# One LayerNorm pass for two in the first stage of a decoder layer, and its splits into high and low parts shared out anew over three engines

## The chip, the cores and the metric

The kernel runs on one core of one Trainium2 chip. The metric is the device time of one execution in microseconds (us); the figure for the kernel before is the median of three runs. A profiled execution beside them gives the trace that all views are drawn from. Five engines work side by side, each in the order of its own list of instructions: PE (TensorE: matmuls; its weight loads are shown as PEld), DVE (VectorE), ACT (ScalarE), POOL (GpSimd) and SP (SyncE, which here issues DMAs).

## The reference, cut to what matters

Inputs are `x` (2 x 2048 tokens of 512 channels), a context, weights. Three blocks follow one another, each on a LayerNorm of its input and added to it: an attention over the rows of two weight matrices, an attention over the context, and a feed-forward part with 32 experts. The change concerns the first block alone:

```
m  = mean(x);   v  = var(x)                      # of each token
r  = (x - m) / sqrt(v + 1e-5)                    # outer LayerNorm
y  = (r - mean(r)) * rsqrt(var(r) + 1e-5)        # inner LayerNorm
q  = (y * ln_g + ln_b), four heads of 128
s  = q @ w_fc.reshape(-1, 128).T                 # 2048 keys for every head
p  = relu(s) ** 2
x1 = x + r + p @ w_proj.T.reshape(-1, 128)
```

The variance of r is v / (v + 1e-5) and its mean is 0. So y is (x - m) times a function of v alone, and x + r is x times one factor plus one offset for each token.

## The kernel before, in words

The program has stages one after another: `stage0` (the block above), `stage1` (attention over the context, and the router), the shared expert, the routed experts. In the profile `stage0` runs from the start to about 822 us of 2793.

**Numbers in parts.** Matmuls take float32r operands. To keep float32 accuracy an operand x is split (`split`, lines 88 to 91 of the listing, L90 and L91 in the profile) into a high part, a cast to float32r, and a low part, x minus the high part; a product is then three matmuls, lo x hi, hi x lo, hi x hi (`three`). In `split` the cast is always on ACT; the subtraction is on DVE, or on POOL where the caller says so.

**Order of the work.** The kernel is written as a list of statements; a scheduler with a model of the engines' times fixes each engine's order when the program is built. `g.after(...)` makes what is emitted within stand behind the named instructions on their engines, `later` lowers the priority. Nothing is reordered at run time.

**stage0.** T = 4096 tokens are worked off in eight tiles t of 512. For each tile there are 4 heads h and 16 blocks kt of 128 keys, so 512 steps (t, h, kt), 64 in a tile. A step has

- three matmuls of 128 x 512 for the scores s (L328), into one of four PSUM banks;
- a relu on ACT (L332, tile rl), and p = s times rl on DVE (L334, tile p, three buffers H);
- the split of p into ph and pl (L339: the cast on ACT, the subtraction on POOL for odd steps and on DVE for even ones);
- the three matmuls with the values (`av`, L289), done for the step LAG = 7 steps earlier.

At the end of a head o is copied by ACT (L293); at the end of a tile it is transposed by PE (L302), x1 is read back, the result added by DVE (L303) and written.

**The LayerNorms** (`prep`, L223 to L259) of tile t + 1 are made during tile t, as two generators of two 128-row tiles each (t = 0: one of four). One generator step is taken per step of the loop from kt = 7 of head 0 on. For each 128-row tile: bn_stats and bn_aggr on DVE (L147, L148); for both together the reciprocal deviation (`rstd`, L132 to L136), a power on POOL and a Newton step in small instructions on DVE; r on DVE (L154); x + r on POOL (L234), written to x1 by SP (L235); then the same statistics of r again, a second `rstd`, a small product nb (L246), and y on ACT (L254). In tile 0 two of the four y are on DVE, and the four x + r stand behind the second power on POOL.

`prep_head` (L261) then transposes y for one head on PE (L264), applies gain and bias on ACT (L266, tile q) and splits q. At the start, before the loop, come the LayerNorms of tile 0, its four heads, and the splits of the two weights: kw (low parts all on POOL) and vw (low parts on DVE, behind `g.mark`, the last y on DVE).

**Background.** From tile 1 on, a step of `context_steps` is taken twice per head: the context's keys and values, and the splitting of further weights (wk, ctx, wv, wq, wo; low parts on POOL).

Of the kernel before, what the change touches and what calls it, by code (L numbers as in the profile page):

```python
# [22 lines left out]
C = 512  # L23
# [5 lines left out]
# Tokens that the expert of each rank (by its number of tokens) has a place for, in blocks of 128 and a last one of 64.  # L29
# [4 lines left out]
# Any further tokens go to blocks of one expert each, worked off in a loop of dynamic length.  # L34
NOV = 64
NBLK = NB + NOV
# Blocks of 128 hidden units of the shared expert that are worked off before the routed ones; the others go between those.
HID = 6
# [6 lines left out]
class Ctx:  # L45
    """The chip's memory in tags that all stages share. Tiles of [128, 512]: A .. K."""
# [25 lines left out]
    def after(self, *instructions):  # L72
        """What is emitted within comes behind these on their engines."""
        stack = ExitStack()
        for i in instructions:
            stack.enter_context(self.tc.issue_after(i.ins))
        return stack


@contextmanager  # L80
def later(g, n):
    """What is traced within stands as far back among the engines' work as if n instructions preceded it."""
    g.tc.cur_priority += n
    yield
    g.tc.cur_priority -= n


def split(g, hi, lo, src, lo_engine=None):
    """src = hi + lo exactly, hi and lo in float32r."""
    g.nc.scalar.copy(hi, src)  # L90
    (lo_engine or g.nc.vector).tensor_tensor(lo, src, f32(hi), A.subtract)  # L91


def split_steps(g, dram, hi, lo, lo_engine=None):
    """A matrix as high and low parts hi[k][c] and lo[k][c] of each 128 rows and their columns, step by step."""
    for k in range(len(hi)):
        at = 0
        for h, l in zip(hi[k], lo[k]):
            n = h.shape[-1]
            raw = g.raw.tile([128, n], F32, name="raw", tag="raw")  # L100
            g.nc.sync.dma_start(raw[:], dram[k * 128:(k + 1) * 128, at:at + n])
            split(g, h, l, raw[:], lo_engine)
            at += n
        if at > 256 or k % 2:
            yield
# [8 lines left out]
def part(w, k, c):  # L114
    """128 columns of 128 rows."""
    return w[k][c // 4][:, c % 4 * 128:c % 4 * 128 + 128]


def run(steps):
    """All of the steps at once, and what they return."""  # L120
    try:
        while True:
            next(steps)
    except StopIteration as end:
        return end.value


def rstd(g, var, n, name):
    """(var + EPS) ** -0.5, a power corrected by a Newton step."""
# [10 lines left out]
def ln_stats(g, xs, name):  # L140
    """Means and reciprocal deviations of the rows of n [128, C] tiles: [128, n, 2] and [128, n], step by step."""
    nc = g.nc
    n = len(xs)
    mv = g.sm.tile([128, n, 2], F32, name=name + "m", tag=name + "m")
    for i, x in enumerate(xs):
        s6 = g.small(name + "s", 6)
        nc.vector.bn_stats(s6[:], x)  # L147
        nc.vector.bn_aggr(mv[:, i, :], s6[:])  # L148
        yield
    return mv, rstd(g, mv[:, :, 1], n, name)  # L150
# [6 lines left out]
def three(terms):  # L157
    """The products of high and low parts that count, smallest first: (w, x) pairs."""
    (wh, wl), (xh, xl) = terms
    return (wl, xh), (wh, xl), (wh, xh)  # L160


# ---------------------------------------------------------------- keys and values of the context
def context_steps(g, ctxT, wk, wv, wq, wo, kst, vst):
    """Keys of two heads as the two blocks of a diagonal, high and low parts of the values side by side; and
    the weights that the attention over them starts with."""
# [46 lines left out]
# ---------------------------------------------------------------- attention over the weights' rows  # L213
def stage0(g, x, wfcT, wpT, lnT, x1, background):
# [8 lines left out]
    def prep(t, tiles):  # L223
        """The steps of two LayerNorms of some 128 tokens each; the first only loads them."""
        rows = [slice(t * 512 + s * 128, t * 512 + s * 128 + 128) for s in tiles]
        xt = [g.tile("G", "xt") for _ in rows]
# [3 lines left out]
        mv, rs = yield from ln_stats(g, [v[:] for v in xt], "a")  # L230
        rt = []

        def add(i):
            nc.gpsimd.tensor_tensor(xt[i][:], xt[i][:], rt[i][:], A.add)  # L234
            nc.sync.dma_start(x1[rows[i], :], xt[i][:])  # L235

        for i, v in enumerate(xt):
            r = g.tile("C", "r")
            normalise(g, r[:], v[:], mv, rs, i)
            rt.append(r)  # L240
            if t > 0:
                add(i)
            yield
        mv, rs = yield from ln_stats(g, [v[:] for v in rt], "b")
        nb = g.small("nb", len(rt))
        nc.vector.scalar_tensor_tensor(nb[:], mv[:, :, 0], -1.0, rs[:], A.mult, A.mult)  # L246
        for i, r in enumerate(rt):
            y = r
            if t == 0:
                y = g.tile("DI"[i % 2], "y")  # L250
            if t == 0 and i % 2:
                g.mark = normalise(g, y[:], r[:], mv, rs, i)
            else:
                nc.scalar.activation(y[:], r[:], AF.Identity, bias=nb[:, i:i + 1], scale=rs[:, i:i + 1])  # L254
            ys[t] = ys.get(t, []) + [y]
        if t == 0:
            with g.after(g.pow):
                for i in range(4):
                    add(i)  # L259

    def prep_head(t, h):  # L261
# [4 lines left out]
        nc.scalar.activation(q[:], pt[:], AF.Identity, bias=gb[:, 1, h:h + 1], scale=gb[:, 0, h:h + 1])  # L266
# [4 lines left out]
    run(prep(0, range(4)))  # L271
    prep_head(0, 0)
    kw = run(weight_steps(g, wfcT, 4, 512, "kw", nc.gpsimd))
    prep_head(0, 1)
    with g.after(g.mark):
# [33 lines left out]
    for i, (t, h, kt) in enumerate(steps):  # L309
# [29 lines left out]
        split(g, ph[:], pl[:], p[:], nc.gpsimd if i % 2 else None)  # L339
# [6 lines left out]
# ---------------------------------------------------------------- attention over the context, router  # L346
def stage1(g, x1, mask, kst, vst, gate, x2, zT, xs, ef, background):
# [4 lines left out]
    def transposed(rows, name, tags="BBEF", banks=("P4", "P4")):  # L352
        """High and low parts of the transpose of two [128, C] tiles: hi[c][:, k, :] has rows 256 c + 128 k of it."""
# [11 lines left out]
    def prep(t):  # L365
        """Loads, then the LayerNorm, then its transpose."""
# [79 lines left out]
    def turn(t, q4):  # L446
        """Probabilities of two pairs of heads transposed."""
# [12 lines left out]
    def values(t, q4, h):  # L460
        """Of one head of each pair: high and low parts of its values are side by side in one operand."""
# [18 lines left out]
    def outputs(t, q4):  # L480
        """The part of the output's product that comes from two pairs of heads."""
# [9 lines left out]
    def finish(t):  # L491
        """What comes of the output, step by step."""
# [91 lines left out]
# ---------------------------------------------------------------- where each token goes  # L584
def bc(ap, axis, n):
    """A broadcast dimension of n at that place of [128, k]."""
# [4 lines left out]
def route(g, ef, tab, tri, ids, plan, idx):  # L591
    """Lists of tokens by block: expert of each rank, expert of each further block, their number."""
# [34 lines left out]
    # Rows of each tile before a token with its expert, and of all tiles before it.  # L627
# [14 lines left out]
    # Experts by their number of tokens.  # L642
# [12 lines left out]
    # Blocks beyond those places, and where each expert's begin.  # L655
# [17 lines left out]
    # Of each token: its block and its place therein.  # L673
# [37 lines left out]
# ---------------------------------------------------------------- the expert of all tokens  # L711
def shared_weights(g, wg, wu, wd):
    """Of the layer's first HID blocks of 128 hidden units as pieces of 512 or 256 columns, and of its rest."""
# [74 lines left out]
# ---------------------------------------------------------------- the rest of the expert of all tokens  # L788
class Rest:
    """The steps of its work on the b-th 256 tokens."""  # L790
# [59 lines left out]
# ---------------------------------------------------------------- the experts of a part of the tokens  # L850
def routed(g, xs, rest, plan, idx, wg, wu, wd, out):
# [10 lines left out]
    # The tags that weights come from in turn: of hidden units, of the output, and as they are loaded.  # L862
# [25 lines left out]
    # Of two blocks of 128 tokens the hidden layer is made in its transpose, with the weights as the standing operand.  # L888
    # Of a block of 64 tokens the high and low parts stand side by side as one operand of 128 columns, so that
    # two passes make all products; the results of the parts are added as they leave the PSUM.  # L890
# [9 lines left out]
    def turned(x, m, bank, tags):  # L900
        """The transpose of [m, 512] in high and low parts, by pieces of 128 rows: two operands, or one of both."""
# [111 lines left out]
    # Units of the shared expert's rest stand between experts: their weights need no loading.  # L1013
# [80 lines left out]
# ---------------------------------------------------------------- blocks beyond the experts' places  # L1094
# [46 lines left out]
def constants():  # L1141
    """Tables that depend on shapes alone."""
# [11 lines left out]
def build(tc, I, out):  # L1154
    from contextlib import ExitStack
    nc = tc.nc
    with ExitStack() as outer:
# [11 lines left out]
        with ExitStack() as inner:  # L1169
            g = Ctx(tc, inner)  # L1170
            g.ident = ident[:]
            g.mhalf = g.c.tile([128, 4], F32, name="mhalf")
# [51 lines left out]
```

## Time and profile before

| | us |
|---|---|
| runs | 2786.57, 2788.44, 2792.36 |
| median | 2788.44 |
| span of the profiled execution, first to last instruction | 2793.2 |
| busy in the span: PE | 2690.4 (96%) |
| DVE | 2071.6 (74%) |
| ACT | 1845.3 (66%) |
| POOL | 962.1 (34%) |
| busy from 36 to 780 us: PE | 719.9 of 744 |
| DVE | 641.9 |
| ACT | 613.4 |
| POOL | 435.9 |
| mean granted clock of PE | 0.990 |

For the profiled execution the profile gives the span only, no time of its own beside it; the span lies 4.8 us above the median of the runs and 0.8 above the slowest of them. A matmul's record ends where a model puts it: full matmuls of 512 columns start 0.227 us after each other but show some 0.39 us each, so a busy share of PE hides short gaps, and the number of entries in a stretch tells more. Some records of matmuls can be missing.

Durations of single instructions in `stage0`, mean of the group, 128 x 512 unless said:

| instruction | engine | ns |
|---|---|---|
| p, L334 | DVE | 684 |
| pl, L91 (256 of them) | DVE | 792 |
| pl, L91 (256 of them) | POOL | 1345 |
| ph cast, L90 | ACT | 621 |
| relu, L332 | ACT | 601 |
| bn_stats, L147 | DVE | 680 and 673 |
| r, L154 | DVE | 778, median 543 |
| y, L254 | ACT | 807 |
| x + r, L234 | POOL | 1451 |
| power of 128 x 2, L133 | POOL | 959 and 860 |

### The profile page before, as it was taken

What the parts mean: (1) busy time and instruction counts of PE and PEld (TensorE: products, weight loads), DVE (VectorE), ACT (ScalarE), POOL (GpSimd) and SP (SyncE); (2) the same over time, 40 slices, a digit from 0 to 9 for tenths busy, and PEclk for the clock granted to TensorE, in tenths of its full rate; (3) what the DMA queues carried; (4) which work ended last, traced back from release to release, by engine and by line L of the source; (5) the groups of instructions that cost most, each with busy time, mean ns of one, the idle gap of its engine ahead of it and who ended that gap; (6) DMA issues with size and microseconds to landing.
All of it is one profiled execution on the core that took longest, in us unless ns stands there. A gap on an engine that the chain in (4) does not pass through costs nothing. (4 is left out here: it accounts for less than half of the span.)

```text
span 2793.2 us, 47704 instructions
## 1 busy us (share of the span) xinstructions
PE 2690.4 (96%) x14788; PEld 2308.8 (83%) x14788; DVE 2071.6 (74%) x4765; ACT 1845.3 (66%) x4089; POOL 962.1 (34%) x774
## 2 busy tenths in 40 slices
PE   5999999999999999999999999999999999999997
PEld 4877877877878999899988888888888988887786
DVE  8898888888887888888877522145677677778885
ACT  5887887887867777777774111135566666667774
POOL 5475465566543333333330120002122222222222
PEclk9999999999999999999999999999999999999999
DMA  3022122122120223222245322255788889988994
GB/s 132 23 76 72 65 69 69 65 62 75 36 81 21 88 74 115 92 85 77 84 144 184 110 91 86 90 175 157 255 275 268 271 270 286 285 268 260 298 304 143
DMA packets 238002, 396.71 MB, mean 142 GB/s; under 512 B 29376, under 2 KB 67280, under 8 KB 237744
## 3 DMA queue, kind: packets, MB, share of 16 engines
q1 hardware_dynamic: 223024, 366.45, 39.4%
q0 software_dynamic: 14720, 27.19, 5.1%
q8 instruction: 117, 1.92, 0.3%
q14 instruction: 141, 1.16, 0.1%
HBM read 311.67 MB, written 83.83 MB: 142 GB/s over the span
## 5 line engine op out<-in xcount | busy, mean ns | idle before, releaser
L91 DVE TENSOR_TENSOR rl<-raw,rh 128x512 fp32r<-128x512 f32 x768 | 513.8, 713 | 134.5 <-ACT rh L90 129.5
L90 ACT CAST rh<-raw 128x512 fp32r<-128x512 f32 x768 | 447.4, 621 | 159.0 <-DMA raw<-in_rg 97.7
L91 POOL TENSOR_TENSOR pl<-p,ph 128x512 fp32r<-128x512 f32 x256 | 344.2, 1345 | 301.0 <-ACT ph L90 282.1
L334 DVE TENSOR_TENSOR p<-s,rl 128x512 f32<-128x512 f32 x512 | 344.4, 684 | 72.2 <-ACT rl L332 67.9
L90 ACT CAST ph<-p 128x512 fp32r<-128x512 f32 x512 | 317.2, 621 | 98.1 <-DVE p L334 75.9
L332 ACT ACTIVATE rl<-s 128x512 f32<-128x512 f32 x512 | 304.0, 601 | 28.1 <-PE s L328 25.4
L439 ACT ACTIVATE e<-e,nm 128x128 f32<-128x128 f32 x512 | 199.2, 391 | 57.4 <-DVE nm L436 56.8
L1010 POOL DMA_INDIRECT out_dram<-v,idx x46 | 91.3, 1984 | 411.5 <-ACT v L1008 276.6
L328 PE MATMUL s<-qh,kwl 128*128 128x512 f32 x512 | 207.3, 406 | 17.9 <-DVE p L334 17.9
L91 DVE TENSOR_TENSOR pl<-p,ph 128x512 fp32r<-128x512 f32 x256 | 202.7, 792 | 25.8 <-ACT ph L90 20.9
L442 POOL TENSOR_TENSOR e<-e,ri 128x512 f32<-128x512 f32 x128 | 133.3, 1042 | 238.2 <-DVE ri L440 144.5
L289 PE MATMUL o<-pl,vwh 128*128 128x512 f32 x512 | 205.1, 401 | 9.7 <-DVE pl L91 8.5
L289 PE MATMUL o<-ph,vwl 128*128 128x512 f32 x512 | 201.7, 394 | 0.0
L328 PE MATMUL s<-qh,kwh 128*128 128x512 f32 x512 | 200.6, 392 | 0.0
L328 PE MATMUL s<-ql,kwh 128*128 128x512 f32 x512 | 200.5, 392 | 0.0
L289 PE MATMUL o<-ph,vwh 128*128 128x512 f32 x512 | 200.3, 391 | 0.0
L896 POOL DMA_INDIRECT x<-xs,idx x46 | 55.5, 1208 | 360.4 <-DMA raw<-in_ru 170.9
L90 ACT CAST hh<-s 128x512 fp32r<-128x512 f32 x92 | 57.1, 620 | 147.6 <-DVE s L751 120.1
L413 PE MATMUL q<-yh,wql 128*128 128x256 f32 x512 | 149.2, 291 | 2.0 <-DVE v L472 1.8
L413 PE MATMUL q<-yh,wqh 128*128 128x256 f32 x512 | 145.5, 284 | 0.0
L413 PE MATMUL q<-yl,wqh 128*128 128x256 f32 x512 | 144.8, 283 | 0.0
L746 PE MATMUL u<-z,sw 128*128 128x512 f32 x576 | 140.0, 390 | 0.0
(291 smaller groups left out, 7707.4 us busy)
## 6 DMA issues: line engine op xcount, KB each, us to landing
raw<-in_rg SPq DMA_DIRECT2D x256, 256.0 KB, 5.3
raw<-in_ru SPq DMA_DIRECT2D x256, 256.0 KB, 5.8
raw<-in_rd SPq DMA_DIRECT2D x256, 256.0 KB, 4.4
z<-zT SPq DMA_DIRECT2D x128, 256.0 KB, 4.9
b<-x SPq DMA_DIRECT2D x64, 256.0 KB, 2.7
xt<-in_x SPq DMA_DIRECT2D x32, 256.0 KB, 2.7
x<-xt SPq DMA_DIRECT2D x32, 256.0 KB, 2.0
x<-b SPq DMA_DIRECT2D x32, 256.0 KB, 2.0
```

Source lines behind the costliest of these rows:

```text
L90: g.nc.scalar.copy(hi, src)
L91: (lo_engine or g.nc.vector).tensor_tensor(lo, src, f32(hi), A.subtract)
L289: nc.tensor.matmul(o[:], w, y[:], start=kt == 0 and n == 0, stop=kt == 15 and n == 2)
L328: nc.tensor.matmul(s[:], w, y[:], start=n == 0, stop=n == 2)
L332: m0 = nc.scalar.activation(r[:], s[:], AF.Relu)
L334: m1 = nc.vector.tensor_tensor(p[:], s[:], r[:], A.mult)
L413: nc.tensor.matmul(o[:, i, :], part(w, k, p), y[k // 2][:, k % 2, :], start=n == 0, stop=n == 11)
L439: nc.scalar.activation(e[:, hs], e[:, hs], AF.Exp, bias=nm[:, h:h + 1], scale=0.125, accum_out=su[:, h:h + 1])
L442: nc.gpsimd.tensor_tensor(e4, e4, ri[:].unsqueeze(2).to_broadcast([128, 4, 128]), A.mult)
L746: nc.tensor.matmul(p[:], part(w, k, c), y[k][:], start=n == 0, stop=n == 11)
L896: nc.gpsimd.indirect_dma_start(out=x[rows], out_offset=None, in_=xs, in_offset=bass.IndirectOffsetOnAxis(ap=idx[rows, b + j:b + j + 1], ax ...
L1010: nc.gpsimd.indirect_dma_start(out=out, out_offset=bass.IndirectOffsetOnAxis(ap=idx[rows, b + j:b + j + 1], axis=0), in_=v[rows], in_offse ...
```

## The change

- `prep` takes one set of statistics, of x. From the variance two columns are made (v + eps, and v (1 + eps) + eps squared), one power of double width gives both deviations, and one Newton step corrects both. y comes straight from x, for all tiles on DVE; the y of ACT, the tile r and the second statistics are gone. x + r becomes one tensor_scalar on POOL, with a factor and an offset for each row from two small DVE instructions; it stands behind the power on POOL.
- y lies in the buffers C in every tile. A pair of 128-row tiles takes five generator steps instead of seven.
- `split` can put the cast on another engine, and can take its low parts' engine from a cycle.
- In the loop, of eight steps, the low part is on POOL for 1, 3, 5, 6 and 7 (before: 1, 3, 5, 7), on DVE for 0, 2 and 4; the cast of step 2 is on DVE instead of ACT.
- At the start kw's low parts alternate between DVE and POOL and its splits stand before the first head; the splits of vw stand behind the second head's q on ACT instead of behind the last y on DVE.
- The table of exponents is eight wide instead of four.

```diff
-def split(g, hi, lo, src, lo_engine=None):
-    g.nc.scalar.copy(hi, src)
+def split(g, hi, lo, src, lo_engine=None, hi_engine=None):
+    if isinstance(lo_engine, cycle):
+        lo_engine = next(lo_engine)
+    if hi_engine is None:
+        g.nc.scalar.copy(hi, src)
+    else:
+        hi_engine.tensor_copy(hi, src)
     (lo_engine or g.nc.vector).tensor_tensor(lo, src, f32(hi), A.subtract)
...
     def prep(t, tiles):
...
-        mv, rs = yield from ln_stats(g, [v[:] for v in xt], "a")
-        rt = []
-        def add(i):
-            nc.gpsimd.tensor_tensor(xt[i][:], xt[i][:], rt[i][:], A.add)
-            nc.sync.dma_start(x1[rows[i], :], xt[i][:])
+        mv = g.sm.tile([128, n, 2], F32, name="am", tag="am")
         for i, v in enumerate(xt):
-            r = g.tile("C", "r")
-            normalise(g, r[:], v[:], mv, rs, i)
-            rt.append(r)
-            if t > 0:
-                add(i)
+            s6 = g.small("as", 6)
+            nc.vector.bn_stats(s6[:], v[:])
+            nc.vector.bn_aggr(mv[:, i, :], s6[:])
             yield
-        mv, rs = yield from ln_stats(g, [v[:] for v in rt], "b")
-        nb = g.small("nb", len(rt))
-        nc.vector.scalar_tensor_tensor(nb[:], mv[:, :, 0], -1.0, rs[:], A.mult, A.mult)
-        for i, r in enumerate(rt):
-            y = r
-            if t == 0:
-                y = g.tile("DI"[i % 2], "y")
-            if t == 0 and i % 2:
-                g.mark = normalise(g, y[:], r[:], mv, rs, i)
-            else:
-                nc.scalar.activation(y[:], r[:], AF.Identity, bias=nb[:, i:i + 1], scale=rs[:, i:i + 1])
+        ve, r0, tt, rs = (g.small("a" + z, 8) for z in "vptr")
+        m = 2 * n
+        nc.vector.tensor_scalar(ve[:, 0:n], mv[:, :, 1], EPS, None, A.add)
+        nc.vector.tensor_scalar(ve[:, n:m], mv[:, :, 1], 1.0 + EPS, EPS * EPS, A.mult, A.add)
+        power = nc.gpsimd.tensor_tensor(r0[:, 0:m], ve[:, 0:m], g.mhalf[:, 0:m], A.pow)
+        nc.vector.scalar_tensor_tensor(tt[:, 0:m], r0[:, 0:m], -0.5, ve[:, 0:m], A.mult, A.mult)
+        nc.vector.tensor_tensor(tt[:, 0:m], tt[:, 0:m], r0[:, 0:m], A.mult)
+        nc.vector.scalar_tensor_tensor(rs[:, 0:m], tt[:, 0:m], 1.5, r0[:, 0:m], A.add, A.mult)
+        for i, v in enumerate(xt):
+            y = g.tile("C", "y")
+            g.mark = nc.vector.tensor_scalar(y[:], v[:], mv[:, i, 0:1], rs[:, n + i:n + i + 1], A.subtract, A.mult)
             ys[t] = ys.get(t, []) + [y]
-        if t == 0:
-            with g.after(g.pow):
-                for i in range(4):
-                    add(i)
+            if i % 2:
+                yield
+
+        sc, of = g.small("bv", 4), g.small("bp", 4)
+        nc.vector.tensor_scalar(sc[:, 0:n], rs[:, 0:n], 1.0, None, A.add)
+        nc.vector.scalar_tensor_tensor(of[:, 0:n], mv[:, :, 0], -1.0, rs[:, 0:n], A.mult, A.mult)
+        for i, v in enumerate(xt):
+            with g.after(power):
+                g.kept = nc.gpsimd.tensor_scalar(v[:], v[:], sc[:, i:i + 1], of[:, i:i + 1], A.mult, A.add)
+            nc.sync.dma_start(x1[rows[i], :], v[:])
+            if i % 2:
+                yield
...
-        nc.scalar.activation(q[:], pt[:], AF.Identity, bias=gb[:, 1, h:h + 1], scale=gb[:, 0, h:h + 1])
+        g.q = nc.scalar.activation(q[:], pt[:], AF.Identity, bias=gb[:, 1, h:h + 1], scale=gb[:, 0, h:h + 1])
...
     run(prep(0, range(4)))
+    steps = weight_steps(g, wfcT, 4, 512, "kw", cycle((nc.vector, nc.gpsimd)))
+    kw = run(steps)
     prep_head(0, 0)
-    kw = run(weight_steps(g, wfcT, 4, 512, "kw", nc.gpsimd))
     prep_head(0, 1)
-    with g.after(g.mark):
+    with g.after(g.q):
         vw = run(weight_steps(g, wpT, 4, 512, "vw"))
...
-        split(g, ph[:], pl[:], p[:], nc.gpsimd if i % 2 else None)
+        split(g, ph[:], pl[:], p[:], nc.gpsimd if i % 8 in (1, 3, 5, 6, 7) else None, nc.vector if i % 8 == 2 else None)
...
-            g.mhalf = g.c.tile([128, 4], F32, name="mhalf")
+            g.mhalf = g.c.tile([128, 8], F32, name="mhalf")
```

More of the change, by code (lines that the diff above doesn't have):

```diff
@@ L225, in prep @@
         rows = [slice(t * 512 + s * 128, t * 512 + s * 128 + 128) for s in tiles]
+        n = len(rows)
         xt = [g.tile("G", "xt") for _ in rows]
```

## The prediction

> **What bounds the kernel now.** I read three views, in this order: the table of busy time by windows over one token tile of the first stage, the list of waits between 36 and 780 us, and the timelines of the first 36 us. The windows first (busy us and count of each engine, then granted clock, DMA share, GB/s):
>
> ```profile
> core 0: us, PE busy (x) PEld busy (x) DVE busy (x) ACT busy (x) POOL busy (x), PEclk, DMA share, GB/s
> 400.00:420.00 20.00, 20.00 (x91) 16.49 (x90) 16.39 (x24) 17.80 (x33) 12.24 (x10) 1.00 0.12 40
> 420.00:440.00 20.00, 20.00 (x91) 16.51 (x90) 16.68 (x27) 15.98 (x31) 10.53 (x8) 1.00 0.12 39
> 440.00:460.00 20.00, 18.43 (x86) 14.48 (x85) 19.99 (x43) 14.23 (x27) 12.33 (x11) 1.00 0.33 107
> 460.00:480.00 20.00, 17.94 (x80) 14.03 (x79) 17.51 (x32) 15.66 (x32) 13.01 (x10) 1.00 0.23 73
> 480.00:500.00 20.00, 20.00 (x92) 16.39 (x91) 15.68 (x37) 17.17 (x43) 7.77 (x6) 1.00 0.12 40
> ```
>
> For most of a tile PE is full: 91 entries in 20 us, matmuls 0.227 us apart. A step (six matmuls) takes 1.36 us, a tile of 64 steps some 90. Only at 440 to 480 does PE thin out, and there DVE is at 19.99 of 20: that is where the LayerNorms of the next tile run. From the records I took how much later than one slot (0.227 us for 512 columns, 0.119 for 256, 0.108 for a transpose) each PE instruction starts after the one before. Up to 830 us that is 55 us: seven bursts, one per LayerNorm of a later tile, of 5.4, 7.5, 6.7, 3.5, 5.3, 4.1 and 9.2 us (41.7 together); 4.8 where the next stage begins; about 4 before 40 us; the rest crumbs. Two bursts hold a dip of the granted clock (0.97 over 50 us, 1.5 us each), so 38.7 us, 5.5 per burst, can be won. Before it lies the start, 30 us without a matmul of the stage proper.
>
> Who ends PE's waits (us in total, times, longest):
>
> ```profile
> PEld s L328 <- DVE p L334: 26.2, 31, 1.4
> PE s L328 <- DVE p L334: 14.7, 23, 0.9
> PEld o L289 <- DVE pl L91: 12.7, 12, 2.1
> PE o L289 <- DVE pl L91: 8.1, 9, 1.6
> PEld o L289 <- POOL pl L91: 2.5, 4, 1.0
> PE o L289 <- POOL pl L91: 1.1, 2, 0.6
> ```
>
> PE and its weight load show the same waits twice; what matters is the name: DVE, hardly POOL. So DVE in the bursts is the bound, and at the start a chain:
>
> ```profile
> 8.04 0.17 DVE L132 TENSOR_SCALAR av<-am 128x4 f32<-128x4 f32 x1
> 11.93 1.19 DVE L136 SCALAR_TENSOR_TENSOR ar<-at,ap 128x4 f32<-128x4 f32 x1
> 13.16 2.81 DVE L154 TENSOR_SCALAR r<-xt,am,ar 128x512 f32<-128x512 f32 x4
> 15.89 1.87 DVE L147 BATCH_NORM_STATS2 bs<-r 128x6 f32<-128x512 f32 x3
> 23.81 1.19 DVE L246 SCALAR_TENSOR_TENSOR nb<-bm,br 128x4 f32<-128x4 f32 x1
> 24.92 0.99 DVE L154 TENSOR_SCALAR y<-r,bm,br 128x512 f32<-128x512 f32 x2
> ```
>
> First scales at 13.1, second scales only at 25.0, first transpose at 25.9, first relu at 32.6.
>
> **The start.** The second chain (15.9 to 25.0) goes. Up to the power nothing changes but one more 0.17 us instruction and a width of 8 for 4. A DVE half of kwl (0.68) falls between the small steps, each of which stands at 1.2 us beside POOL. New scales at about 13.5, four y at 0.54 to 0.70 each, the last at 16.3 against 26.5: 10 to 11 us earlier. Given back: the vwh casts now stand between ACT's q and qh, four at 0.56 before the first relu, where before two ran in the idle time at 11.3 and two while PE transposed: 2.2 us at most. I take 9; 5 and 11.5 are the ends.
>
> **The bursts.** Removed per tile on DVE: four second bn_stats (0.67) and aggregates (0.16), 3.3 us; per pair of 128-row tiles nine small instructions (means 0.36, 0.61, 0.21, 0.26 for the first norm, 0.41, 0.98, 0.31, 0.16, 0.62 for the second), 3.9 us, become seven (0.36 twice, 0.61, 0.21, 0.26, then 0.41, 0.62 for the new scale and offset), 2.8 us. DVE's four normalisations stay, writing y instead of r. That is 3.3 + 2 x 1.1 = 5.5 us of 17.6 per tile. ACT loses four y at 0.81, 3.2 us. One of eight steps also moves its high part from ACT (0.62) to DVE and one low part from DVE (0.68 alone) to POOL. For the DVE copy there is no row; the nearest is the one-input normalisation of the same tile, 0.543 median; the dearer end is the two-input subtraction, 0.684, the cheaper comes from the Trainium skill (VectorE: DVE Perf Modes, The perf-mode tier table), which has an fp32 copy in SBUF at 1227 ns for 2048 elements and a two-input operation at 2293: with the trace's 684 for 512 the latter is 148 ns and 1.05 per element, and at half of that per element the copy would take, as an estimate, 0.42. I take 0.54: DVE gains 0.14 us per eight steps, ACT 0.62, POOL pays 1.30. Outside bursts this is worth nothing, as PE is full there; within, it is a little slack.
>
> In a burst DVE has some 0.95 us of steady work per 1.36 us step and about 0.9 of LayerNorm on top, spread over 14 generator steps: a deficit of 0.5 us per step, 7 us, of which the score banks and the lag of seven steps swallow a part and 5.5 surface. After it a pair takes five steps instead of seven: ten steps at a similar density, 4.8 us of deficit, less the same cushion: about 2 surface. Gain 3.5 us x 7 = 24.5. Ends: 0 (DVE's small instructions wait for POOL as long as ever) and 38.7. What is late next, where it goes, is again p on DVE.
>
> **POOL and its queue.** Per eight steps (10.85 us) POOL's low parts go from four to five, 5.2 to 6.5 us. In its own time there is room. Per tile the second power goes (two at 0.86), and the sum xt + r (1.45 mean, 1.25 least) becomes one tensor_scalar with two scalars. No POOL row has one input of that size but a memset of 0.53; the Trainium skill (GPSIMD Engine Reference, Engine selection) has one-input work at about line rate. The nearest row by operation is the 1.25, so no change; 0.53 and 2.0 are the ends, 4 x 0.75 us per tile on an engine that ends few waits. Behind it on POOL stand pl of the steps, behind those the av matmuls seven steps (9.5 us) later; its write to x1 follows on SP, ahead of the next tile's loads, which have tens of microseconds to spare.
>
> The rule that speaks against the change: the Trainium skill (SBUF — State Buffer, Who interferes with whom) says that a DVE instruction with two SBUF inputs, or a one-input one in a two-port mode, and a GpSimd instruction exclude each other whole. The trace agrees on DVE's side:
>
> ```profile
> 459.97 1.50 POOL L234 TENSOR_TENSOR xt<-xt,r 128x512 f32<-128x512 f32 x1 [1.57 <-DVE r L154]
> 460.26 1.76 DVE L91 TENSOR_TENSOR pl<-p,ph 128x512 fp32r<-128x512 f32 x1
> 461.44 1.72 POOL L91 TENSOR_TENSOR pl<-p,ph 128x512 fp32r<-128x512 f32 x1
> ```
>
> Subtraction 1.76 instead of 0.68, POOL 1.72 instead of 1.30, while p, with one operand in PSUM, never takes more than 0.694 in 512 times. By the rule, the ports they share are taken per eight steps for 4 x 1.30 + 4 x 0.68 = 7.9 us before and 5 x 1.30 + 3 x 0.68 + 0.54 = 9.1 after, of 10.85; where two context weights per eight steps are split on POOL as well, 10.5 before and 11.7 after, 0.85 too many in each of eight such groups: 7 us lost. By the rows the loss is smaller: at 160 to 200, such groups at 97% of the shared ports, PE lost no more than 0.7 us in 10. I take 0, with 7 as the end.
>
> **Sum.** 9 + 24.5 = 33.5 us. The profiled span is 2793.2, 4.8 above the median of the runs (2788.4) and just above the slowest; the sum leaves the span at 2760 and the median at 2755. Later stages move up as they are; the order of the first tiles of the next stage differs in places, worth 2 us either way.
>
> **Rivals.** *Start alone (0.20):* the bursts keep their 5.5 us, since small instructions at 1.2 us and y still queue behind a fuller POOL. For it: alone they take 0.15, on average up to 0.98. Against: there are fewer. 2788.4 - 9 = 2779.
> *POOL takes over (0.09), slower:* steps 5, 6, 7 of eight put three low parts in a row on POOL, and p has three buffers, so DVE's p waits for POOL's third before it. If held-up POOL instructions become the rule, at w us each, the shared ports need 5w + 2.6 per eight steps; beyond w = 1.65 every group overruns, beyond 1.68 the overrun of 64 groups eats the start's 9 us. At 1.80, the longest seen, 0.75 x 64 = 48 us: 2788.4 - 9 + 48 = 2827. Against it: the mean is 1.345.
> *Nothing (0.05):* the start hangs on the weights' loads and splits, not the norms; 2788. Against: kwh is cast by 11.1 us.
> *All bursts vanish (0.04):* 2788.4 - 11 - 38.7 = 2739.
> The likeliest keeps 0.62, with its own range of 2743 to 2768.
>
> **Chances and range.** About 0.2%, 5.6 us, is what can be told from no change, so below 2782.9 is faster: 0.62 + 0.04 + 0.18 of the start-alone case = 0.84; same 0.08; slower 0.08. The range runs from 2739, all bursts gone, to 2783, somewhat worse than the start alone; it leaves out the case of no effect, that of POOL and the edges of the others, 0.17 together.
>
> **What would show it.** First relu near 24 us instead of 32.6; no second bn_stats; windows with a LayerNorm at 84 or more PE entries per 20 us instead of 80 to 86 and DVE below 19; waits of s for p about halved; POOL's pl near 1.35. I am wrong if pl on POOL ends PE's waits or its mean nears 1.6, if DVE's small instructions lengthen, or if the stage's end (822 us) moves by less than 15 us.

## The result, and the profile after

The changed kernel takes 2779.67 us (median of 17 runs, 2769.63 to 2789.82), the kernel before in the same series 2790.55 (17 runs, 2778.33 to 2796.49). The ratio is 0.9969, 95% interval 0.9955 to 0.9982: 8.6 us (5 to 12.5) less, where 33 were forecast. (The two medians lie 10.9 apart, which is within this interval.) The profiled execution took 2778.45 us, with a span of 2776.4. That its span lies 16.8 us below the one before says more than there is: the one before was among the longest of its kernel's, and holds two dips of the granted clock in this stage (3.4 us at half speed each, so 1.7 us lost each), the one after none.

The start came as forecast. This is ACT's timeline of the changed kernel (start, duration, instruction, idle time before it and who ended it):

```profile
15.59 1.45 ACT L274 ACTIVATE q<-pt,gb 128x512 f32<-128x512 f32 x2 [4.29 <-PE pt L272]
16.93 0.61 ACT L93 CAST vwh<-raw 128x512 fp32r<-128x512 f32 x1
22.36 0.63 ACT L93 CAST qh<-q 128x512 fp32r<-128x512 f32 x1
22.88 1.08 ACT L341 ACTIVATE rl<-s 128x512 f32<-128x512 f32 x2
```

The first relu stands at 22.9 us instead of 32.6; the vwh casts lie between ACT's q and qh, as the prediction had them. The windows around the LayerNorms that end tile 4:

```profile
core 0: us, PE busy (x) PEld busy (x) DVE busy (x) ACT busy (x) POOL busy (x), PEclk, DMA share, GB/s
400.00:420.00 20.00, 19.43 (x83) 14.44 (x82) 14.98 (x19) 15.06 (x29) 14.66 (x11) 1.00 0.08 27
420.00:440.00 20.00, 19.79 (x93) 15.30 (x91) 19.18 (x39) 14.34 (x27) 10.63 (x9) 1.00 0.23 80
440.00:460.00 20.00, 18.46 (x79) 13.81 (x78) 16.93 (x30) 12.73 (x25) 15.96 (x14) 1.00 0.35 119
460.00:480.00 20.00, 20.00 (x91) 16.55 (x91) 16.14 (x34) 16.39 (x39) 11.63 (x9) 1.00 0.10 34
```

DVE is at 16.93 instead of 17.5 to 20 of 20 where PE is thin, but PE is as thin as ever (79), and now also at 400 to 420 (83 entries, 19.43), ahead of any LayerNorm, where the kernel before had 91. POOL is at 15.96 of 20. Who ends PE's waits between 28 and 770 us:

```profile
DVE p L343 <- ACT rl L341: 58.0, 114, 1.4
PEld s L337 <- DVE p L343: 16.9, 42, 1.2
PEld o L298 <- DVE pl L96: 14.2, 19, 2.5
DVE p L343 <- POOL pl L96: 14.1, 20, 1.3
PEld o L298 <- POOL pl L96: 10.4, 18, 1.0
PE o L298 <- DVE pl L96: 7.2, 8, 2.0
PE s L337 <- DVE p L343: 4.0, 10, 0.8
PE o L298 <- POOL pl L96: 2.8, 7, 0.6
PE pt L272 <- DVE y L254: 2.0, 2, 1.0
```

The waits for p fell (26.2 to 16.9 on the weight loads), as forecast. In their place stand waits for POOL's pl (2.5 to 10.4), for y, and a wait that the kernel before did not have: DVE's p for POOL's pl, 20 times. And the subtractions on POOL and on DVE, as groups:

```profile
L96 POOL TENSOR_TENSOR pl<-p,ph 128x512 fp32r<-128x512 f32 x320 | 427.9, 1346 | 243.2 <-ACT ph L93 217.7
L96 DVE TENSOR_TENSOR pl<-p,ph 128x512 fp32r<-128x512 f32 x192 | 184.4, 961 | 16.3 <-ACT ph L93 15.0
```

The kernel before had for the second of these:

```profile
L91 DVE TENSOR_TENSOR pl<-p,ph 128x512 fp32r<-128x512 f32 x256 | 202.7, 792 | 25.8 <-ACT ph L90 20.9
```

64 subtractions fewer on DVE, 43.8 us at 0.684, saved only 18.3 us (202.7 to 184.4), since those that remain take 961 ns instead of 792.

One measure serves the experiments: the loop's length, from the start of the first matmul with the values to the end of the last in the records, less what the dips of the granted clock took. Before it is 786.4 us, after 788.0. So the whole gain is the start's; the loop lost what it won.

### The profile page after: what moved, and what is told of

It reads as the page before. It is cut to its first block, busy times and chain, and to the rows that moved or that the text cites. A ratio compares the mean times of both kernels' runs of the same rounds, so it can differ in the third digit from the quotient of the medians.

```text
span 2776.4 us, 47492 instructions
## 1 busy us (share of the span) xinstructions
PE 2694.0 (97%) x14788; PEld 2298.8 (83%) x14788; DVE 2054.5 (74%) x4671; ACT 1793.1 (65%) x3995; POOL 1023.1 (37%) x821
## 5 line engine op out<-in xcount | busy, mean ns | idle before, releaser
L96 POOL TENSOR_TENSOR pl<-p,ph 128x512 fp32r<-128x512 f32 x320 | 427.9, 1346 | 243.2 <-ACT ph L93 217.7
L93 ACT CAST ph<-p 128x512 fp32r<-128x512 f32 x448 | 277.3, 622 | 153.9 <-DVE p L343 148.4
L96 DVE TENSOR_TENSOR pl<-p,ph 128x512 fp32r<-128x512 f32 x192 | 184.4, 961 | 16.3 <-ACT ph L93 15.0
```

## Experiments

Each job timed its kernels against runs of the kernel before on the same chip; e5 to e8 ran on another chip than the other experiments. Chips differ (the kernel before has medians of 2787.9, 2794.3 and 2787.4 us in the three jobs), so I compare ratios to the kernel before, with their 95% intervals; 0.001 is 2.8 us. The loop and the late starts come from one profiled execution of each kernel. "Late starts" are what PE's instructions start later than a slot after the one before, within the loop, worked out as in the prediction and split by who ended the wait.

| kernel | ratio (interval) | loop, us | late starts, us | for p | for DVE's pl | for POOL's pl | for y |
|---|---|---|---|---|---|---|---|
| before | 1 | 786.4 | 51.0 | 25.8 | 11.7 | 2.4 | 0.4 |
| changed | 0.9969 (0.9955 to 0.9982) | 788.0 | 47.2 | 15.5 | 12.1 | 8.6 | 3.8 |
| e11 start alone | 0.9979 (0.9968 to 0.9989) | 787.8 | 54.7 | 26.2 | 14.4 | 2.4 | 0 |
| e1 old sharing | 0.9887 (0.9863 to 0.9912) | 765.0 | 26.9 | 14.6 | 3.0 | 1.6 | 1.0 |
| e2 sharing alone | 1.0068 (1.0046 to 1.0091) | 803.5 | 69.9 | 30.2 | 17.5 | 9.8 | 0.4 |
| e3 no cast on DVE | 0.9912 (0.9890 to 0.9935) | 768.3 | 32.5 | 12.4 | 3.6 | 0.9 | 6.4 |
| e4 cast, four on POOL | 0.9947 (0.9926 to 0.9967) | 781.3 | 42.1 | 15.2 | 13.3 | 5.0 | 2.0 |
| e5 high part from PSUM | 0.9922 (0.9904 to 0.9941) | 775.6 | 35.7 | 11.2 | 7.5 | 4.1 | 3.1 |
| e6 needless bn_stats | 0.9901 (0.9881 to 0.9921) | 771.8 | 33.0 | 14.8 | 7.5 | 2.6 | 1.1 |
| e7 half the casts | 0.9939 (0.9923 to 0.9955) | 779.3 | 40.6 | 14.1 | 4.0 | 4.8 | 9.4 |
| e8 transposes held back | 0.9919 (0.9899 to 0.9938) | 772.6 | 39.5 | 8.0 | 15.7 | 4.1 | 0 |
| e9 y on ACT | 0.9899 (0.9882 to 0.9916) | 763.3 | 26.6 | 10.0 | 5.8 | 3.2 | - |
| e10 POOL spread | 0.9875 (0.9855 to 0.9895) | 760.4 | 23.5 | 6.2 | 4.1 | 1.5 | 2.7 |
| e12 three on POOL | 0.9873 (0.9855 to 0.9891) | 759.1 | 20.8 | 3.4 | 9.4 | 1.0 | 0.8 |

The late starts still hold the time that the clock's dips took; the rest of a row are waits whose end the records do not name.

**First: which part of the change eats the gain?** Theory A was that the loop's new sharing does, through POOL and the ports it shares with DVE; theory B that the bursts stay as they are whatever the sharing.

*e1, the changed kernel with the old sharing:*

```diff
-        split(g, ph[:], pl[:], p[:], nc.gpsimd if i % 8 in (1, 3, 5, 6, 7) else None, nc.vector if i % 8 == 2 else None)
+        split(g, ph[:], pl[:], p[:], nc.gpsimd if i % 2 else None)
```

> The changed kernel with the old sharing of the loop's splits (low part on POOL for odd steps, every cast on ACT); norms and start as changed. Theory A (the fuller POOL and the ports it shares with DVE eat what the norms gain): DVE's pl falls from 961 to near 800 ns, PE's waits for POOL's pl from 8.4 us back to about 2, and the loop gets 10 us or more shorter than in the changed kernel, about 2768 us. Theory B (the bursts stay whatever the sharing, since DVE's small instructions and y set them): within 3 us of the changed kernel, about 2779.

Measured: 2758.5 us, ratio 0.9887, loop 765.0. The windows of e1 over the same stretch as above:

```profile
400.00:420.00 20.00, 20.00 (x95) 16.63 (x94) 17.18 (x31) 16.50 (x32) 10.59 (x9) 1.00 0.17 54
420.00:440.00 20.00, 20.00 (x93) 16.35 (x92) 19.43 (x39) 13.13 (x26) 13.06 (x13) 1.00 0.35 119
440.00:460.00 20.00, 20.00 (x89) 16.54 (x89) 15.72 (x30) 17.75 (x39) 10.57 (x8) 1.00 0.22 67
```

PE is full through the LayerNorms of this tile, though DVE is at 19.43 of 20 there. Its pl is back at 799 ns:

```profile
L96 DVE TENSOR_TENSOR pl<-p,ph 128x512 fp32r<-128x512 f32 x256 | 204.6, 799 | 19.7 <-ACT ph L93 13.2 <-PE o L298 1.2 <-PE s L337 0.3
```

Theory A holds, and B falls: norms and start without the new sharing give what the whole change was forecast to give.

*e2, the kernel before with the new sharing alone:* the same line the other way round, with `hi_engine` in `split`.

> The kernel before with only the new sharing of the loop's splits (five of eight low parts on POOL, one of eight casts on DVE). Theory A: slower than before by 5 to 12 us, about 2799 us, with POOL's pl ending PE's waits for some 6 us more. Theory B: the sharing is harmless or a slight help, 2785 to 2791 us.

Measured: 2810.7 us against 2787.9 before in its job, ratio 1.0068, loop 803.5. The sharing costs 19 us by itself, more than expected. DVE's p waits for POOL's pl here too:

```profile
PEld s L330 <- DVE p L336: 31.3, 42, 2.3
PEld o L291 <- DVE pl L93: 19.4, 21, 2.1
DVE p L336 <- POOL pl L93: 15.3, 25, 1.2
PEld o L291 <- POOL pl L93: 12.0, 20, 1.8
```

**Second: the fifth low part on POOL, or the cast on DVE?**

*e3, all casts back on ACT:*

```diff
-        split(g, ph[:], pl[:], p[:], nc.gpsimd if i % 8 in (1, 3, 5, 6, 7) else None, nc.vector if i % 8 == 2 else None)
+        split(g, ph[:], pl[:], p[:], nc.gpsimd if i % 8 in (1, 3, 5, 6, 7) else None)
```

> The changed kernel without the cast on DVE: the cast of step 2 of eight back on ACT, five low parts on POOL as changed. If POOL's three low parts in a row do the harm (theory A, part 1): as the changed kernel, within 3 us, POOL's pl still ends some 8 us of PE's waits. If the cast on DVE does it by blocking POOL (part 2): about 2770. Theory B: 2779.

*e4, four low parts on POOL, the cast still on DVE:*

```diff
-        split(g, ph[:], pl[:], p[:], nc.gpsimd if i % 8 in (1, 3, 5, 6, 7) else None, nc.vector if i % 8 == 2 else None)
+        split(g, ph[:], pl[:], p[:], nc.gpsimd if i % 2 else None, nc.vector if i % 8 == 2 else None)
```

> The changed kernel with the cast of step 2 of eight still on DVE but four low parts on POOL (odd steps) as before. Theory A, part 1 (the fifth low part on POOL does the harm): about 2769, PE's waits for POOL's pl near 2 us. Part 2 (the cast on DVE does it): about 2779 or more. Theory B: 2779.

Measured: e3 2762.9 us (0.9912), e4 2775.6 us (0.9947). From e1 the cast alone costs 0.0060, 17 us; the fifth low part alone 0.0025, 7 us, which the intervals don't tell from nothing. From the changed kernel, taking the cast away gives 0.0057, 16 us. So most of the harm, two thirds or more, is the cast's, 64 instructions of 37.6 us in all.

**Third: does the cast cost DVE's time, or POOL's?**

*e5, the same high part by another instruction:* in step 2 of eight

```diff
-        split(g, ph[:], pl[:], p[:], nc.gpsimd if i % 8 in (1, 3, 5, 6, 7) else None, nc.vector if i % 8 == 2 else None)
+        if i % 8 == 2:
+            nc.vector.tensor_tensor(ph[:], s[:], r[:], A.mult)
+            nc.vector.tensor_tensor(pl[:], p[:], f32(ph[:]), A.subtract)
+        else:
+            split(g, ph[:], pl[:], p[:], nc.gpsimd if i % 8 in (1, 3, 5, 6, 7) else None)
```

> The changed kernel with the high part of step 2 of eight made on DVE in another way: s times rl once more, straight from PSUM into float32r (0.68 us, one operand in SBUF), in place of the cast of p. If the cast does its harm by excluding POOL from the shared ports (theory C): as without it, about 2763 us, DVE's pl below 900 ns. If it does it by DVE's time in the bursts (theory D): 2779 or a little more, as the changed kernel, since DVE's load is the same.

Measured: ratio 0.9922, and 0.9969 for the changed kernel; the intervals are apart. It is an instruction of 678 ns in place of one of 588 (means), and the kernel is 13 us faster. The group lines of e5 and then of e4 (the cast with four low parts on POOL):

```profile
L350 DVE TENSOR_TENSOR pl<-p,ph 128x512 fp32r<-128x512 f32 x64 | 48.9, 765 | 0.1
L349 DVE TENSOR_TENSOR ph<-s,rl 128x512 fp32r<-128x512 f32 x64 | 43.4, 678 | 0.0
```

```profile
L95 DVE CAST ph<-p 128x512 fp32r<-128x512 f32 x64 | 45.0, 702 | 3.8 <-DVE p L343 0.5
```

On average the multiplication from PSUM takes 0.68 us and the subtraction behind it 0.77. In the changed kernel the subtraction behind a cast takes 1.04 on average (worked out over the 64 of them in the records), and a cast up to 1.52:

```profile
L95 DVE CAST ph<-p x64: 408/427/1521, 26.5 to 804.2; 128x512 fp32r<-128x512 f32 x64
```

The timelines of DVE and POOL of the changed kernel show how, in the stretch at 395 us where no LayerNorm runs:

```profile
396.66 0.43 DVE L95 CAST ph<-p 128x512 fp32r<-128x512 f32 x1
397.12 1.66 DVE L96 TENSOR_TENSOR pl<-p,ph 128x512 fp32r<-128x512 f32 x1
398.70 1.28 DVE L343 TENSOR_TENSOR p<-s,rl 128x512 f32<-128x512 f32 x2
400.67 1.36 DVE L96 TENSOR_TENSOR pl<-p,ph 128x512 fp32r<-128x512 f32 x1 [0.69 <-ACT ph L93]
...
406.26 1.44 DVE L96 TENSOR_TENSOR pl<-p,ph 128x512 fp32r<-128x512 f32 x1 [0.69 <-ACT ph L93]
```

```profile
396.69 1.54 POOL L96 TENSOR_TENSOR pl<-p,ph 128x512 fp32r<-128x512 f32 x1 [1.88 <-ACT ph L93]
400.17 1.31 POOL L96 TENSOR_TENSOR pl<-p,ph 128x512 fp32r<-128x512 f32 x1 [1.94 <-ACT ph L93]
401.72 1.47 POOL L96 TENSOR_TENSOR wvl<-raw,wvh 128x512 fp32r<-128x512 f32 x1 [0.24 <-ACT wvh L93]
403.36 3.80 POOL L96 TENSOR_TENSOR pl<-p,ph 128x512 fp32r<-128x512 f32 x3 [0.17 <-ACT ph L93]
```

A cast starts; POOL's subtraction comes 0.03 us later, is held for the cast and takes 1.54; DVE's own subtraction comes next, is held until POOL is through at 398.23, and takes 1.66. All four subtractions of DVE from 395 to 412 us take 1.36 or more. That fits a cast that excludes POOL, after which POOL excludes DVE.

*e6, DVE time by another instruction:* e1 and, in step 2 of eight, a bn_stats of p that nobody reads.

```diff
+        if i % 8 == 2:
+            s7 = g.small("xs", 6)
+            nc.vector.bn_stats(s7[:], p[:])
+        split(g, ph[:], pl[:], p[:], nc.gpsimd if i % 2 else None)
```

> The changed kernel with the old sharing (2758.5 us) and one needless bn_stats of p on DVE in step 2 of eight, 64 times 0.68 us, that nobody waits for and that reads SBUF once. Theory C: within 4 us of 2758. Theory D: like four low parts and the cast on DVE, about 2775.

Measured: ratio 0.9901, 0.0014 or 4 us above e1, which the intervals don't tell from nothing, where the cast in the same place (e4) costs 17. About as much DVE time (64 of 0.69 against 64 of 0.70 us), a quarter of the price; by the loops in the table it is 6.8 us of 16.3. So DVE's time has a share, and theory D falls for the larger part: it is the form of the instruction that costs. Theory C, the shared ports, is the reading that fits the timelines. One rival to it is open: each edit also makes the scheduler lay out another fixed order. Of the 64 subtractions of step 2 on DVE, 63 stand one p behind their own in e3 and 59 in e5, but 30 in the changed kernel (worked out from the records). How much of the cast's price is this order was not separated from the ports.

*e7, the cast for heads 2 and 3 only:*

```diff
-        split(g, ph[:], pl[:], p[:], nc.gpsimd if i % 8 in (1, 3, 5, 6, 7) else None, nc.vector if i % 8 == 2 else None)
+        split(g, ph[:], pl[:], p[:], nc.gpsimd if i % 8 in (1, 3, 5, 6, 7) else None, nc.vector if i % 8 == 2 and h >= 2 else None)
```

> The changed kernel with the cast on DVE only for heads 2 and 3 of a tile, where no LayerNorm runs, so 32 times instead of 64. If the harm lies in the bursts: as without the cast, about 2763 us. If a cast costs the same anywhere: half of the harm stays, about 2771.

Measured: ratio 0.9939, halfway between 0.9912 (none) and 0.9969 (all), though its interval overlaps that of e3 and touches that of the changed kernel. The total alone would say that a cast costs the same anywhere; the place of the loss in the tile does not. From the starts of the score matmuls, with the clock's dips taken off and the first 16 steps left out, this is how much longer than in e3 the steps of all tiles take together:

| kernel | steps 0 to 7 of a tile | 8 to 31 (LayerNorms) | 32 to 63 (heads 2 and 3) |
|---|---|---|---|
| changed, 64 casts | 2.5 us | 11.9 | 4.1 |
| e7, 32 casts, all in heads 2 and 3 | 2.3 | 5.4 | 3.4 |

So in heads 2 and 3, where both kernels have the same casts, some 4 us are lost, and two thirds of the changed kernel's loss lie where the LayerNorms run. Half of e7's loss lies there too, where it has no cast; why is open (its waits for y are 9.4 us against 6.4, and its order is another). What I held of the stretches outside the bursts, that PE is full there and nothing is lost, is wrong, but the larger part is lost within.

**Fourth: the rest, and better versions.**

*e11, the first term alone:* the new LayerNorm for tile 0 and the new order at the start; `prep` of before for later tiles, and the old sharing.

```diff
-            todo = [prep(t + 1, tiles) for tiles in ((0, 1), (2, 3))]
+            todo = [prep_later(t + 1, tiles) for tiles in ((0, 1), (2, 3))]
```

> The new LayerNorm for tile 0 and the new order of the weights' splits at the start, everything else (LayerNorms of later tiles, the loop's sharing) as before. The first term of the sum alone: first relu near 23 us, the loop as long as before, ratio to the kernel before 0.9965 (9 to 10 us). If the start's gain is eaten later: 0.999 or more.

Measured: 0.9979, 6 us (3 to 9). The first relu comes 9.0 us earlier, the first matmul with the values 8.3, and the loop is 1.4 us longer.

*e8, e3 with the transposes of y held back* behind the score matmuls of the step before. The scheduler puts most of them at steps 14 to 23 of a tile, where the LayerNorms run; written they stand at 28, 44, 60 and 8 of the next tile. The last is held back in the same way.

```diff
-            prep_head(t + 1, h - 1)
+            with g.after(g.mm):
+                prep_head(t + 1, h - 1)
...
-            nc.tensor.matmul(s[:], w, y[:], start=n == 0, stop=n == 2)
+            g.mm = nc.tensor.matmul(s[:], w, y[:], start=n == 0, stop=n == 2)
```

> The changed kernel without the cast on DVE (2762.9 us), and the transposes of y held back to their own step in the written order (steps 28, 44, 60 and 72), where the scheduler has them at steps 16 to 24, among the LayerNorms. If PE's 6.4 us of waits for y and part of those for p come from that crowding: 2750 to 2757 us and no wait for y. If they only move: 2763.

Measured: 0.9919, as e3 (0.9912): a miss. The 6.4 us of waits for y are gone and those for p fell from 12.4 to 8.0, but those for DVE's pl rose from 3.6 to 15.7. They moved.

*e9, e1 with y of the later tiles on ACT,* from x with a scale and an offset:

```diff
...
-            g.mark = nc.vector.tensor_scalar(y[:], v[:], mv[:, i, 0:1], rs[:, n + i:n + i + 1], A.subtract, A.mult)
+            if t > 0:
+                nc.scalar.activation(y[:], v[:], AF.Identity, bias=nb[:, i:i + 1], scale=rs[:, n + i:n + i + 1])
+            else:
+                nc.vector.tensor_scalar(y[:], v[:], mv[:, i, 0:1], rs[:, n + i:n + i + 1], A.subtract, A.mult)
```

> The changed kernel with the old sharing in the loop (ratio 0.989) and y of tiles 1 to 7 on ACT instead of DVE. If DVE still sets the bursts: 3 to 6 us less again, ratio 0.987. If ACT, then busy some 95% of the stage, or PE's early transposes set them: 0.989 or more.

Measured: 0.9899, as e1: the 3 to 6 us did not come. Taking 16 us off DVE (busy 670 to 655 us up to the loop's end) gives nothing that the runs can tell.

*e10, e3 with POOL's five low parts spread:*

```diff
+        split(g, ph[:], pl[:], p[:], nc.gpsimd if i % 8 in (0, 2, 3, 5, 7) else None)
```

> The changed kernel without the cast on DVE and with its five low parts on POOL spread (steps 0, 2, 3, 5, 7: two in a row at most) instead of 1, 3, 5, 6, 7 (ratio 0.991). If three in a row with three buffers of p matter: 0.988, no wait of DVE's p for POOL. If it is the number that counts, not their place: 0.991.

Measured: 0.9875, 10 us less than e3; the two intervals just overlap. The wait of DVE's p for POOL's pl between 28 and 770 us, first in e3, then in e10:

```profile
DVE p L343 <- POOL pl L96: 15.8, 24, 1.3
```

```profile
DVE p L343 <- POOL pl L96: 3.7, 5, 0.8
```

That fits three in a row using up the three buffers of p; five on POOL, spread, cost nothing that the runs can tell from e1.

*e12, three low parts on POOL and five on DVE:*

```diff
+        split(g, ph[:], pl[:], p[:], nc.gpsimd if i % 8 in (1, 3, 6) else None)
```

> The changed kernel with every cast on ACT and only three of eight low parts on POOL (steps 1, 3, 6), five on DVE. If what counts is how often the two engines meet at their shared ports: pl on DVE waits less, under 760 ns, and the time is about that of four (ratio 0.989). If DVE's own time counts: 64 more subtractions, 44 us of DVE, cost 8 us or more, 0.992 or above.

Measured: 2750.1 us, 0.9873, a loop of 759.1, the shortest of all, though five of eight subtractions are DVE's: up to the loop's end DVE is busy 689 us, as in the changed kernel (689) and 48 more than in e3 (641), whose loop is 9 us longer. DVE's pl takes 777 ns, a little over what was expected. Both e10 and e12 beat the kernel before by some 35 us and the changed kernel by some 26; they are not told apart from each other or from e1.

## Why the prediction was wrong, point by point

**The start: mechanism right, size somewhat high.** 9 us were forecast. In the changed kernel the first score matmul stands 11.8 us earlier and the first relu 9.7, so what goes back to the casts is 2.1, as forecast; e11 has 6 (3 to 9) in the end.

**The bursts: right.** From e11 to e1 only the LayerNorms of the later tiles change: 0.0092, 26 us, and the loop goes from 787.8 to 765.0, 22.8 us. 24.5 were forecast. With the start, e1's 0.0113 is 31.5 us against 33.5. That waits for DVE would fall is shown (the late starts for p and for DVE's pl are 17.6 us in e1, 40.6 in e11). That the size comes so near is in part luck, as the sum has two slips that pull opposite ways: 17.6 us over 14 steps are 1.26 a step, not 0.9, and a cushion of 7 - 5.5 = 1.5 leaves 3.3 of 4.8, not 2. With its own figures 0.85 over 14 steps becomes 0.80 over ten, 3.9 us less in a burst and 27 in all.

**What failed is the sharing.** The step reads: "Outside bursts this is worth nothing, as PE is full there; within, it is a little slack", and for the shared ports "I take 0, with 7 as the end". It is worth +23 us (e1 to the changed kernel, 0.0082; +19 alone, in e2). By place, the steps 8 to 31 of the tiles, where the "little slack" was to be, are 13 us longer than in e1, the others 8. Three things in the step were wrong. DVE's gain was worked out with the durations of instructions that meet nothing: the subtraction moved off DVE at 0.684, the cast at 0.54. The ones that stay pay for it: 192 at 961 ns instead of 792 are 32 us more. Then, "PE is full there" was taken to mean that nothing can be lost there. PE full says only that the engines that feed it are in time; at 400 us they no longer are. Last, the load of the shared ports was summed over eight steps (9.1 of 10.85 us) and found to fit. A sum does not see single meetings: in the timeline at 396 us a cast of 0.43 us leaves POOL's subtraction behind it at 1.54 instead of 1.30 us, and DVE's next subtraction behind that one at 1.66 instead of 0.68. e5 against the changed kernel shows that it is this form of instruction, not its time alone. The prediction named four signs of being wrong, and two came: POOL's pl ends PE's waits (10.4 us on the weight loads), and the stage's end moved by 10.8 us (824.9 to 814.1). The mean of POOL's pl stayed at 1.346, and the small instructions did not lengthen in sum.

**The rivals.** The start alone has the time that came (2779), but not the reason: its bursts were to stay because small instructions wait, and e1 shows that they go. The rival that lost time to POOL named a wait that came, "DVE's p waits for POOL's third before it": 14.1 us of waits in 20 cases, 15.8 in e3, and 3.7 in e10 without the run of three. It priced it as an overrun of the ports at w beyond 1.65 per POOL instruction, where the mean stayed at 1.346; so the price, 48 us, did not come, and some 10 did (e3 to e10, intervals that touch). The rule of the Trainium skill that speaks against the change (SBUF — State Buffer, Who interferes with whom) was the right one to weigh, and "By the rows the loss is smaller" was the wrong verdict: the rows came from stretches without a cast, and they were read too well. From 160 to 170 us PE's instructions start 3.6 us late in sum (a LayerNorm ends there too), from 170 to 200 0.8, 0.7 and 0 us in each 10. Even the rule's own sum gave 7 us where 23 came.

**Single costs.** The cast alone takes 0.427 us (median). The estimate from the Trainium skill (VectorE: DVE Perf Modes, The perf-mode tier table) was 0.42 and fits; I took 0.54. The sum x + r on POOL takes 0.870 (mean) instead of 1.25. The small instructions per pair add up as forecast, though the single ones do not: 0.29, 0.16, 0.87, 0.76, 0.30, 0.32 and 0.15 are 2.84 us for 2.8.

**Left open.** Why the transposes' waits for y come and go between kernels that differ only in the sharing; how much of the cast's price is the ports and how much the other order that the scheduler makes with it; how much of the changed kernel's loss the run of three has beside the cast's, since no kernel has the cast with a spread POOL.

## What to carry to other kernels

Before work is moved between VectorE and GpSimd to even out their busy times, look in the timelines at what each of the two takes while the other is busy, not at its duration alone. Here a product read from PSUM (e5) and a bn_stats (e6) on VectorE beside a busy GpSimd cost 3 and 4 us in 64 instructions, and a float32 cast between two SBUF tensors 16 to 17. Where GpSimd takes every n-th item, count the buffers against its longest run; spreading its items gave 10 us here, with intervals that just overlap. Time an edit that shifts load and one that removes work as two kernels: here the first ate three quarters of what the second gained.

## What the runs showed of the hardware that was not expected

- A power on POOL takes longer the wider it is, few as its elements are: group means of 0.70 to 0.96 us for 128 x 2 and 1.01 to 1.40 for 128 x 4, and 1.67 and 2.17 for the single ones of 128 x 8 (before, changed, e1).
- A tensor_scalar with two scalars per row on POOL takes 0.78 us (median) for 128 x 512, against 1.30 for a two-input subtraction.
- A float32 copy to float32r on DVE takes 0.43 us (median), a tensor_scalar with two scalars per row of the same size 0.54.
- e12, with three low parts on POOL, has the shortest loop (759.1 us) with DVE busy for 689 us of the 785.5 up to its end; e3 has 641 of 797.8 and a loop of 768.3. Here busy time on DVE was no measure of what the engine costs.
